# Soft mixture of experts: combine's sums over experts by halves, its first logits fetched into the places of the normed tokens, and the last slot groups and combine in written order

## The chip, the cores and the metric

The kernel runs on one core of one Trainium2 chip. The metric is the time of one execution on the device in microseconds, taken as the median of several runs. The core has a matrix engine (PE), a vector engine (DVE), an activation engine (ACT), a general engine (POOL) and an engine that issues transfers (SP). Each of them runs its own list of instructions in the order of that list, and they meet at semaphores. All arithmetic is in float32.

## The reference

Four layers work on 16 sequences of 128 tokens with 256 features, each layer a gated cross attention and a gated feed-forward part. The change lies in the feed-forward part of layer 2, a soft mixture with 64 experts of 32 slots each:

```python
logits = (jnp.einsum('tzd,ed->tze', x, phi_w) + phi_b).reshape(t, z, n, p)
D = jax.nn.softmax(logits, axis=3)
C = jax.nn.softmax(logits, axis=2)
X_tilde = jnp.einsum('tznp,tzd->npd', D, x)
X_tilde = jnp.clip(X_tilde, -33000.0, 65000.0)
...
X_tilde = (X_tilde - mu) * jax.lax.rsqrt(var + LN_EPS)
X_tilde = jnp.tanh(X_tilde)
Y_tilde = jnp.einsum('npd,ndH->npH', X_tilde, expert_w) + expert_b[:, None, :]
Y = jnp.einsum('tznp,npH->tzH', C, Y_tilde)
```

Here x is the normed input, n = 64 experts and p = 32 slots. So every token has 2048 logits. The same logits are used twice: D is a softmax over the 32 slots of one expert, and C is a softmax over the 64 experts for one slot number. The result Y is scaled by a gate and added to the residual.

## The kernel before

The 2048 tokens are 16 blocks of 128, one token to a partition. The feed-forward part of layer 2 is the function `attention_ffn2`. After the attention of layer 2 it has three stages.

**Dispatch** (`dispatch` and `gather`, lines 1246 to 1288) runs 32 steps: first the logits of the first 1024 columns for all 16 blocks, then those of the other 1024. In a step PE computes two times 512 logits from the transposed normed tokens (`xnT`, four tiles of four blocks each) and the weights `phi`; DVE adds the bias, and SP writes the 1024 logits to a buffer in memory (`spill`). DVE then takes the maximum over the 32 slots (`red`), the maximum over the experts of this half (`top`, line 1266), and subtracts `red`; ACT takes the exponential, DVE sums and inverts, POOL multiplies. Two steps later `gather` multiplies the result on PE with the normed tokens and adds it up in four banks; after the last block of a half ACT copies them to `xtT`.

**Slots** (`slots_norm`, `slots_turn`, `slots_expert`, lines 1182 to 1229) has eight groups of 256 slots. For each group PE turns the slots, DVE clamps them and takes their statistics, POOL computes the inverse root (`rsqrt`, lines 190 to 195), ACT applies tanh, PE turns them again, ACT copies, and PE multiplies with the weights of eight experts. DVE adds the bias to give `yt`. Groups 0 to 3 belong to the first half and are spread over dispatch steps 18 to 29. Groups 4 to 7 come after the last gather. The expert weights (2 MB a group) are loaded into the pool `wp`, which has four places that `phi`, expert weights, fetched logits and the weights of attention 3 share.

**Combine** (`combine`, `turn`, `spread`, lines 1306 to 1342) reads the logits back from memory, two blocks (2 MB) to a place of `wp` (`fetch`, line 1234). For each block DVE subtracts the maximum over the experts (line 1311), ACT takes the exponential in four pieces (line 1315), DVE sums the 2048 values over the 64 experts (line 1317), inverts (1318) and scales (1319). Then each quarter of a block, called a unit here, is turned on PE by four transposes (line 1325), copied by ACT (1329), and multiplied with `yt` in four matrix products (1337). In the profile each product counts as two matmuls. After four units DVE adds the gated result to the residual (line 259). PE spreads a unit two units after it has turned it.

In these stages the order of instructions on each engine is made by a scheduler from priorities, from the order of the program and from free places of the pools; it is not written out. A block `tc.manual_schedule(engines=ENGINES)` fixes the order on PE, ACT, DVE and POOL to the one in which the program states it; the feed-forward part of layer 3 is already written so. Transfers on SP are never part of such a block. Instructions of later stages may still be placed between those of a block: two of these matter here, the preparation of the key mask of attention 3 (line 1632, which needs the mask that line 1628 loads) and the statistics and norm of the residual for attention 3 (lines 199, 201 and 226).

Attention 3 (`xattn64`, lines 269 to 408) follows. Its weights are loaded over POOL's queue into places of `wp`.

## Time and profile before

| What | Value |
|---|---|
| Time before, median of 3 runs | 2056.13 us (2055.76 to 2060.23) |
| Profiled execution, its own time | 2059.8 us |
| Its span, first to last instruction | 2058.1 us |
| PE busy over the span | 1854.9 us (90%) |
| DVE busy | 1257.9 us (61%) |
| ACT busy | 912.3 us (44%) |
| POOL busy | 791.2 us (38%) |
| Granted PE clock, mean | 0.952 |
| Spread matmuls, line 1337 | 126.1 us for 512 |
| Last gather ends, about | 1318.6 us from the start |
| First turn of combine | 1353.07 us |
| First projection of attention 3 (line 287) | 1513.9 us |

Times inside the kernel are counted from the first instruction of the profiled execution. A line of the profile names an engine, a line of the program, an operation, output and inputs, and shapes. Busy time is not the time an engine costs: what counts is who waits last, and the idle time in brackets behind a line names the instruction whose end it was put down to. The column for the PE clock is the share of the full clock that was granted.

### The profile page before, as it was taken

What the parts mean: (1) busy time and instruction counts of PE and PEld (TensorE: products, weight loads), DVE (VectorE), ACT (ScalarE), POOL (GpSimd) and SP (SyncE); (2) the same over time, 40 slices, a digit from 0 to 9 for tenths busy, and PEclk for the clock granted to TensorE, in tenths of its full rate; (3) what the DMA queues carried; (4) which work ended last, traced back from release to release, by engine and by line L of the source; (5) the groups of instructions that cost most, each with busy time, mean ns of one, the idle gap of its engine ahead of it and who ended that gap; (6) DMA issues with size and microseconds to landing.
All of it is one profiled execution on the core that took longest, in us unless ns stands there. A gap on an engine that the chain in (4) does not pass through costs nothing.

```text
span 2058.1 us, 31016 instructions
## 1 busy us (share of the span) xinstructions
PE 1854.9 (90%) x10345; PEld 1242.7 (60%) x10345; DVE 1257.9 (61%) x3763; ACT 912.3 (44%) x3002; POOL 791.2 (38%) x952
## 2 busy tenths in 40 slices
PE   6996899979879999989979989868999999998787
PEld 3774566557636566657744434357776677775775
DVE  3885122478752222249859999699717666663797
ACT  4993222489911222249931122244324434333673
POOL 4873332377510455448832222200102222220785
PEclk9997999998889999999999999989999999999799
DMA  3003777310010688861031123433200000000000
GB/s 118 14 17 111 283 292 283 113 31 27 17 75 1 252 321 315 308 230 37 2 115 79 75 109 143 181 144 120 82 1 1 1 1 1 22 1 1 6 17 21
DMA packets 52720, 204.19 MB, mean 99 GB/s; under 512 B 11600, under 2 KB 31568, under 8 KB 41552
## 3 DMA queue, kind: packets, MB, share of 16 engines
q0 software_dynamic: 13872, 121.12, 16.1%
q1 hardware_dynamic: 38688, 81.07, 11.2%
q8 instruction: 84, 1.38, 0.3%
q14 instruction: 76, 0.62, 0.1%
HBM read 171.75 MB, written 30.41 MB: 98 GB/s over the span
## 4 chain that ended last, share of the span: by engine, by line
PE 27%; DVE 20%; issue 3%; ACT 3%; POOL 2%; DMA 1%; SPq 0%; POOLq 0%; ACTq 0%; DVEq 0%
PE pk L287 3%; PE pq L299 3%; PE po L382 3%; PE pv L310 3%; DVE tot L1317 2%; DVE rep L1523 2%; PE acc L1280 2%; PE po L1337 2%; PE av L372 2%; DVE cw L1311 1%; PE sc L329 1%; PE pq L1419 1%; DVE cw L1319 1%; PE pe L358 1%; PE pl L1254 1%
## 5 line engine op out<-in xcount | busy, mean ns | idle before, releaser
L922 PE MATMUL pg<-we,xT 128*128 128x512 f32 (+1 forms) x528 | 243.1, 590 | 2.4 <-ACT xT L211 2.4
L579 POOL TENSOR_TENSOR e<-e,sums 128x512 f32<-128x512 f32 x192 | 199.6, 1071 | 67.4 <-DVE sums L574 28.4
L928 DVE TENSOR_TENSOR h<-sg,pg 128x256 f32<-128x256 f32 x132 | 54.3, 411 | 237.7 <-ACT sg L927 190.1
L566 ACT ACTIVATE e<-sc,mx 128x128 f32<-128x128 f32 x512 | 181.5, 421 | 17.3 <-DVE mx L544 16.3
L927 ACT ACTIVATE sg<-pg 128x256 f32<-128x256 f32 x132 | 49.7, 376 | 270.3 <-PE pg L922 260.3
L888 POOL DMA_INDIRECT we<-in_we,rows x56 | 54.0, 964 | 265.6 <-PE pd L953 165.2
L350 POOL TENSOR_TENSOR e<-e,rec 128x512 f32<-128x512 f32 x64 | 65.3, 1041 | 219.0 <-DVE rec L349 155.2
L922 PEld LDWEIGHTS pg<-we,xT 128*128 128x128 f32 x528 | 96.2, 194 | 82.2 <-issue 72.1
L1337 PE MATMUL po<-yt,cT 128*128 128x256 f32 x512 | 126.1, 391 | 11.2 <-ACT cT L1329 11.1
L1280 PE MATMUL acc<-d,k 128*128 128x512 f32 x256 | 123.1, 623 | 13.9 <-POOL d L1270 13.5
L566 ACT ACTIVATION_READ_ACCUMULATOR e<-sc,mx 128x1 f32 x512 | 132.9, 260 | 0.0
L585 PE MATMUL pe<-ident,e 128*128 128x128 f32 x768 | 103.7, 279 | 32.0 <-DVE mx L549 17.4
L1270 POOL TENSOR_TENSOR d<-d,tot 128x1024 f32<-128x1024 f32 x32 | 62.8, 1961 | 174.0 <-DVE tot L1269 174.0
L953 PE MATMUL pd<-we,hT 128*128 128x256 f32 x528 | 127.2, 383 | 1.2 <-ACT hT L942 1.2
L1265 ACT ACTIVATE d<-d 128x1024 f32<-128x1024 f32 x32 | 33.8, 1057 | 200.8 <-DVE d L1264 178.9
L953 PEld LDWEIGHTS pd<-we,hT 128*128 128x128 f32 x528 | 98.4, 190 | 40.0 <-issue 23.7
L585 PEld LDWEIGHTS pe<-ident,e 128*128 128x128 f32 x768 | 86.0, 142 | 49.9 <-POOL e L579 24.6
L1254 PE MATMUL pl<-phi,xnT 128*128 128x512 f32 x256 | 116.1, 598 | 0.0
L1337 PEld LDWEIGHTS po<-yt,cT 128*128 128x128 f32 x512 | 95.6, 197 | 23.8 <-ACT cT L1329 12.6
L566 ACT ACTIVATE e<-e,mx 128x128 f32<-128x128 f32 x256 | 99.0, 397 | 0.3 <-DVE mx L549 0.3
L259 DVE SCALAR_TENSOR_TENSOR x<-po,gates,x 128x256 f32<-128x256 f32 x96 | 42.6, 444 | 92.5 <-PE po L382 54.2
L1280 PEld LDWEIGHTS acc<-d,k 128*128 128x128 f32 x256 | 48.9, 199 | 78.7 <-issue 53.3
(304 smaller groups left out, 4361.5 us busy)
## 6 DMA issues: line engine op xcount, KB each, us to landing
ew<-in_ew SPq DMA_DIRECT2D x8, 2048.0 KB
spill<-lg SPq DMA_DIRECT2D x32, 512.0 KB
cw<-spill SPq DMA_DIRECT2D x8, 2048.0 KB
got<-results SPq DMA_DIRECT2D x48, 128.0 KB
normed<-xn SPq DMA_DIRECT2D x32, 128.0 KB
aw<-in_aw SPq DMA_DIRECT2D x6, 512.0 KB
ctxT<-in_ctxT SPq DMA_DIRECT2D x4, 512.0 KB
x<-in_x SPq DMA_DIRECT2D x16, 128.0 KB
```

Source lines behind the costliest of these rows:

```text
L287: nc.tensor.matmul(pk, lhsT=wk[:, k, c * P : (c + 1) * P], rhs=ctxT[g][:, k, :], start=(k == 0), stop=(k == 1))
L299: nc.tensor.matmul(pq[:, i * gt : (i + 1) * gt], lhsT=wq[:, k, (c + i) * P : (c + i + 1) * P], rhs=xnTs[g][:, k, :], start=(k == 0), stop= ...
L350: nc.gpsimd.tensor_tensor(e, e, rec.unsqueeze(2).to_broadcast([P, 4, S]), ALU.mult)
L566: nc.scalar.activation(e[:, c, :], sc[:, c, :], AF.Exp, bias=mx[:, h : h + 1], scale=sign, accum_out=sums[b][:, h : h + 1],)
L579: nc.gpsimd.tensor_tensor(e, e, r, ALU.mult)
L585: nc.tensor.transpose(pe[:, c * P : (c + 1) * P], e[:, c, :], ident)
L922: nc.tensor.matmul(pg[:, 0 : 2 * m].rearrange("p (g i) -> p g i", g=2), lhsT=tokens[j][:, k, :], rhs=wgu[:, k, :, i0 : i0 + m], start=(k = ...
L953: nc.tensor.matmul(pd[:, 0:D], lhsT=hT[0:m, ic, :], rhs=wd[0:m, ic, :], start=(ic == 0), stop=(ic == nic - 1))
L1254: nc.tensor.matmul(pl, lhsT=xnT[b // 4][:, k, tok], rhs=phi[:, k, n], start=(k == 0), stop=(k == 1))
L1270: nc.gpsimd.tensor_tensor(dv, dv, tot.unsqueeze(2).to_broadcast([P, 32, 32]), ALU.mult)
L1280: nc.tensor.matmul(acc[hf][k][q], lhsT=keep[b][:, k * P : (k + 1) * P], rhs=d[:, q * 512 : (q + 1) * 512], start=(b == 0), stop=(b == B - 1),)
L1337: nc.tensor.matmul(pos[b][:, 0:D], lhsT=cT[:, c, :], rhs=yt[2 * q + c // 2][:, c % 2, :], start=(q == 0 and c == 0), stop=(q == 3 and c == 3),
```

## The change

It has five parts.

1. `slots_norm` is split into `slots_gather` (up to the inverse root) and `slots_squash` (from there on).
2. The logits of blocks 0 and 1 are not fetched into `wp`, but in four pieces of 1024 columns into the four places of the normed tokens (`fetch_early`), each as its place comes free in the second half of dispatch. The other blocks are fetched as before, now with one transfer to a block.
3. `combine` is split into four functions. The maximum of the two halves of `top` is taken once for all blocks. The sum over experts adds the two halves of the 2048 columns, then the two halves of the result, and reduces the remaining 512 columns.
4. The last dispatch step, the last gathers, the slot groups 4 to 7, and pieces of combine for blocks 0 and 1 are in one written order.
5. The loop of combine is in a written order too, with the exponentials one piece to a unit, and the shift, the sum and the scaling of a block each at one of the units before it.

```diff
-            def slots_norm(n, dp):
+            def slots_gather(n, dp):
...
                 rsqrt(rs, mv[:, :, 1], 1e-5)
+                xs[n] = t, mv, rs
+
+            def slots_squash(n, dp):
+                t, mv, rs = xs[n]
                 nm = small.tile([P, 2], F32, tag="nm2", name="nm2")
...
+            def fetch_early(b):
+
+                cws[b] = []
+                for h in range(2):
+                    t = xtp.tile([P, 2, GT], F32, tag="xnT", name="cwe").rearrange("p c t -> p (c t)")
+                    nc.sync.dma_start(out=t, in_=spill[b, :, h * 1024 : (h + 1) * 1024])
+                    cws[b].append(t)
+
             def fetch(n):
 
                 cw = wp.tile([P, WSLOT], F32, tag="w", name="cw")[:, 0:4096].rearrange("p (i m) -> p i m", i=2)
-                nc.sync.dma_start(out=cw, in_=spill[2 * n : 2 * n + 2].rearrange("i p m -> p i m"))
                 for i in range(2):
-                    cws[2 * n + i] = cw[:, i, :]
+                    nc.sync.dma_start(out=cw[:, i, :], in_=spill[2 * n + i])
+                    cws[2 * n + i] = [cw[:, i, :]]
...
+            def combine_shift(b):
+                for part in cws[b]:
+                    cv = part.rearrange("t (n p) -> t n p", p=32)
+                    nc.vector.tensor_tensor(
+                        cv, cv, top[:, b, 0, :].unsqueeze(1).to_broadcast([P, cv.shape[1], 32]), ALU.subtract
+                    )
+
+            def combine_exp(b, q):
+                part = logits_of(b, q * 512, 512)
+                nc.scalar.activation(part, part, AF.Exp)
+
+            def combine_sum(b, pool):
+
+                t = pool.tile([P, 1024], F32, tag="lg", name="tree", bufs=2)
+                nc.vector.tensor_tensor(t, logits_of(b, 0, 1024), logits_of(b, 1024, 1024), ALU.add)
+                nc.vector.tensor_tensor(t[:, 0:512], t[:, 0:512], t[:, 512:1024], ALU.add)
+                tots[b] = small.tile([P, 32], F32, tag="tot32", name="tot")
+                nc.vector.tensor_reduce(tots[b], t[:, 0:512].rearrange("t (n p) -> t p n", p=32), AX.X, ALU.add)
+
+            def combine_scale(b):
+                tot = tots.pop(b)
+                nc.vector.reciprocal(tot, tot)
+                for part in cws[b]:
+                    cv = part.rearrange("t (n p) -> t n p", p=32)
+                    nc.vector.tensor_tensor(
+                        cv, cv, tot.unsqueeze(1).to_broadcast([P, cv.shape[1], 32]), ALU.mult
+                    )
...
-                for t in range(2 * B + 2):
-                    if t < 2 * B:
-                        dispatch(t)
+                for t in range(2 * B - 1):
+                    dispatch(t)
...
-                pipeline(4, *(lambda n, stage=stage: stage(4 + n, dp) for stage in slots))
-                fetch(0)
+                    if t == 2 * B - 8:
+                        fetch_early(0)
+
+
+                with tc.manual_schedule(engines=ENGINES):
+                    dispatch(2 * B - 1)
+                    fetch_early(1)
+                    gather(2 * B - 3)
+                    gather(2 * B - 2)
+                    nc.vector.tensor_tensor(top[:, :, 0, :], top[:, :, 0, :], top[:, :, 1, :], ALU.max)
+                    combine_shift(0)
+                    for q in range(4):
+                        combine_exp(0, q)
+                    gather(2 * B - 1)
+                    combine_shift(1)
+                    for q in range(3):
+                        combine_exp(1, q)
+                    combine_sum(0, dp)
+                    for n in (4, 5):
+                        slots_gather(n, dp)
+                    for n in (4, 5):
+                        slots_squash(n, dp)
+                    combine_scale(0)
+                    slots_turn(4, dp)
+                    slots_gather(6, dp)
+                    slots_turn(5, dp)
+                    slots_gather(7, dp)
+                    slots_expert(4, dp)
+                    fetch(1)
+                    for n in (6, 7):
+                        slots_squash(n, dp)
+                    slots_expert(5, dp)
+                    for n in (6, 7):
+                        slots_turn(n, dp)
+                    for n in (6, 7):
+                        slots_expert(n, dp)
...
+                with tc.manual_schedule(engines=ENGINES):
+                    for u in range(4 * B + 4):
+                        b, q = divmod(u, 4)
+                        if q == 0 and b % 2 == 0 and b + 4 < B:
+                            fetch(b // 2 + 2)
+                        if u < 4 * B:
+                            turn(u)
+                        if q == 0 and b + 1 < B:
+                            combine_exp(b + 1, 3)
+                        if q > 0 and b + 2 < B:
+                            combine_exp(b + 2, q - 1)
+                        if 0 <= u - 2 < 4 * B:
+                            spread(u - 2)
+                        if q == 0 and b + 2 < B:
+                            combine_shift(b + 2)
+                        if q == 1 and b + 1 < B:
+                            combine_sum(b + 1, cp)
+                        if q == 2 and b + 1 < B:
+                            combine_scale(b + 1)
+                        if q == 2 and b > 0:
+                            add_gated(b - 1, pos.pop(b - 1)[:, 0:D], gate_f(2))
```

`logits_of(b, at, n)` gives n columns of block b's logits from column `at` on, whichever of the two forms of storage the block has.

More of the change, by code (lines that the diff above doesn't have):

```diff
@@ L1229, in slots_expert, with slots_norm @@
                 nc.vector.tensor_tensor(yt[n], py.rearrange("p (i d) -> p i d", i=2), yt[n], ALU.add)
+            def slots_norm(n, dp):
+                slots_gather(n, dp)
+                slots_squash(n, dp)
             slots = (slots_norm, slots_turn, slots_expert)
             cws = {}
+            def fetch_early(b):
[4 more added lines that the diff above has]
+                    cws[b].append(t)
@@ L1234, in fetch, with logits_of @@
             def fetch(n):
                 cw = wp.tile([P, WSLOT], F32, tag="w", name="cw")[:, 0:4096].rearrange("p (i m) -> p i m", i=2)
-                nc.sync.dma_start(out=cw, in_=spill[2 * n : 2 * n + 2].rearrange("i p m -> p i m"))
                 for i in range(2):
-                    cws[2 * n + i] = cw[:, i, :]
+                    nc.sync.dma_start(out=cw[:, i, :], in_=spill[2 * n + i])
+                    cws[2 * n + i] = [cw[:, i, :]]
+            def logits_of(b, at, n):
+                parts = cws[b]
+                size = 2048 // len(parts)
+                return parts[at // size][:, at % size : at % size + n]
@@ new lines, in attention_ffn2 @@
+            tots = {}
+            def combine_shift(b):
[13 more added lines that the diff above has]
+                nc.vector.tensor_reduce(tots[b], t[:, 0:512].rearrange("t (n p) -> t p n", p=32), AX.X, ALU.add)
@@ L1298, in attention_ffn2 @@
                         gather(t - 2)
-                pipeline(4, *(lambda n, stage=stage: stage(4 + n, dp) for stage in slots))
-                fetch(0)
+                    if t == 2 * B - 8:
[15 more added lines that the diff above has]
+                    for n in (4, 5):
+                        slots_gather(n, dp)
+                    for n in (4, 5):
[8 more added lines that the diff above has]
+                    for n in (6, 7):
+                        slots_squash(n, dp)
+                    slots_expert(5, dp)
[3 more added lines that the diff above has]
+                        slots_expert(n, dp)
@@ L1303, in attention_ffn2 @@
             with tc.tile_pool(name="comb", bufs=3) as cp:
                 cTs, pos = {}, {}
-                def combine(b):
-                    cw = cws[b]
-                    cv = cw.rearrange("t (n p) -> t n p", p=32)
-                    red = cp.tile([P, 32], F32, tag="red", name="red")
-                    nc.vector.tensor_tensor(red, top[:, b, 0, :], top[:, b, 1, :], ALU.max)
-                    nc.vector.tensor_tensor(cv, cv, red.unsqueeze(1).to_broadcast([P, 64, 32]), ALU.subtract)
-                    for q in range(4):
-                        part = cw[:, q * 512 : (q + 1) * 512]
-                        nc.scalar.activation(part, part, AF.Exp)
-                    tot = cp.tile([P, 32], F32, tag="tot", name="tot")
-                    nc.vector.tensor_reduce(tot, cv.rearrange("t n p -> t p n"), AX.X, ALU.add)
-                    nc.vector.reciprocal(tot, tot)
-                    nc.vector.tensor_tensor(cv, cv, tot.unsqueeze(1).to_broadcast([P, 64, 32]), ALU.mult)
@@ L1325, in turn @@
                         nc.tensor.transpose(
-                            pt[:, c * P : (c + 1) * P], cws[b][:, (4 * q + c) * P : (4 * q + c + 1) * P], ident
+                            pt[:, c * P : (c + 1) * P], logits_of(b, (4 * q + c) * P, P), ident
                         )
@@ L1340, in spread @@
                         )
-                    if q == 3:
-                        add_gated(b, pos.pop(b)[:, 0:D], gate_f(2))
-                fetch(1)
-                for b in range(2):
-                    combine(b)
-                for u in range(4 * B + 2):
-                    b, q = divmod(u, 4)
-                    if q == 0:
-                        if b % 2 == 0 and b + 4 < B:
-                            fetch(b // 2 + 2)
-                        if b + 2 < B:
-                            combine(b + 2)
-                    if u < 4 * B:
-                        turn(u)
-                    if u >= 2:
-                        spread(u - 2)
+                with tc.manual_schedule(engines=ENGINES):
+                    for u in range(4 * B + 4):
+                        b, q = divmod(u, 4)
+                        if q == 0 and b % 2 == 0 and b + 4 < B:
+                            fetch(b // 2 + 2)
+                        if u < 4 * B:
[14 more added lines that the diff above has]
+                            add_gated(b - 1, pos.pop(b - 1)[:, 0:D], gate_f(2))
     def attention_ffn3():
```

## The prediction

> **What bounds the kernel now.** I read the page first (PE busy 90% of the span), then the stretches around the changed stage, the timelines of PE and DVE in it, the chain, and the waits of the DMA queue. Busy time per stretch (columns: stretch, length, busy us of PE, weight load, DVE, ACT, POOL, PE clock, DMA share, GB/s):
>
> ```profile
> 1311.00:1338.00 27.00, 19.10 (x168) 10.54 (x168) 9.76 (x32) 8.99 (x16) 5.46 (x9) 0.87 0.38 147
> 1338.00:1353.00 15.00, 0.00 (x0) 0.00 (x0) 15.00 (x13) 4.38 (x8) 0.00 (x0) 0.57 0.81 335
> 1353.00:1470.00 117.00, 104.23 (x552) 90.37 (x552) 117.00 (x79) 51.93 (x98) 0.77 (x2) 0.97 0.24 90
> 1470.00:1514.00 44.00, 43.11 (x217) 37.55 (x218) 12.49 (x27) 12.75 (x23) 6.37 (x17) 0.92 0.13 49
> ```
>
> From 1338 to 1470 DVE is busy without a gap: combine is bound by DVE, PE stands still for 15 us and then waits in places. From 1470 PE works off what is left. PE's timeline:
>
> ```profile
> 1313.51 5.09 PE L1280 MATMUL acc<-d,k 128*128 128x512 f32 x8 [3.11 <-POOL d L1270]
> ...
> 1353.07 2.79 PE L1325 MATMUL pt<-ident,cw 128*128 128x128 f32 x12 [15.50 <-DVE cw L1319]
> ...
> 1470.89 3.78 PE L1337 MATMUL po<-yt,cT 128*128 128x256 f32 x8 [2.97 <-ACT cT L1329]
> ```
>
> The first turn of combine starts at 1353.07, held by the division of DVE. Eight spread matmuls take 3.78 us after an idle gap of 2.97, against 1.73 when fed, which the chain shows:
>
> ```profile
> 1486.60 0.44 PE pt L1325 x4
> 1487.03 1.73 PE po L1337 x8
> ```
>
> So a unit (a quarter of a block) costs PE 2.17 us; 64 units are 138.7 us. The chain hands over to attention 3 at 1513.9: combine takes 160.8. Now DVE ahead of it, and the mask load of attention 3 on SP:
>
> ```profile
> 1305.58 1.90 DVE L1266 TENSOR_REDUCE top<-lg 128x32 f32<-128x1024 f32 x1
> 1307.39 1.21 DVE L1264 TENSOR_TENSOR d<-lg,red 128x1024 f32<-128x1024 f32 x1
> 1309.79 1.22 DVE L1268 TENSOR_REDUCE tot<-d 128x32 f32<-128x1024 f32 x1 [1.18 <-ACT d L1265]
> 1311.05 0.35 DVE L1269 RECIPROCAL tot<-tot 128x32 f32<-128x32 f32 x1
> 1319.08 1.29 DVE L1193 TENSOR_SCALAR xs<-pt 128x512 f32<-128x512 f32 x2 [7.68 <-PE pt L1189]
> ```
> ```profile
> SPq L1628 <- PE acc L1280: 13.9, 1, 13.9
> ```
> ```profile
> 1318.64 0.33 SPq L1628 DMA_DIRECT2D mk<-in_mask_k  x1
> ```
>
> DVE has a hole of 7.68 us while PE ends the dispatch; the mask waits for the last gather.
>
> **Part 1: first blocks of combine into the dispatch tail.** The four early fetches (512 KB each) stand on SP behind spills 18, 22, 26 and 30, and wait for the matmuls of dispatch 19, 23, 27, 31, which end before the logits that the next spill needs: no spill or expert load behind them is held by that wait. Their bytes take 1.3 us each at the 400 GB/s of the fetch stretch. A logits buffer is reused two dispatches (some 15 us) later, and after its start this stage shows no DVE wait on a spill: 0, bounds 0 to 4 x 1.3 = 5.2 us (the one row against is the wait of 8.0 us in the third dispatch, at 1071 to 1079).
>
> In dispatch 31 the written order puts the subtraction ahead of the column maximum. Start to start the maximum is 1.81, and 1.18 was waited for the exponential, so the division is ready some 1.2 us earlier: POOL ends at 1312.1 instead of 1313.45. PE's gap before the last gather falls from 3.11 to about 1.7. Gaps of 2.38 and 2.73 left the matmuls at speed, those of 2.97 and more did not; so I take 3.6 us instead of 5.09 (bounds 3.6 to 5.1) and an end at 1315.7 instead of 1318.6.
>
> DVE meanwhile, from 1310.0: maximum over the halves (512 elements, by the 512-wide add at L1229, 0.6), shifts of blocks 0 and 1 (4 x 1.13, by L1264), the sum of block 0 as 1.13 + 0.6 + 0.95 (a half, a quarter, and a 512-element reduction at the 3.63/2048 of L1317): 7.9 us, in the hole of 7.68. The exponentials (4 x 0.52 on ACT) end at about 1314.1; the copies of the accumulators queue behind them and still end with the last accumulator. The sixteen small maxima of L1310 (0.1 to 0.2 each) go.
>
> **The wait it adds.** In the issue order of the changed kernel one mask preparation (0.15 us, L1632 before) comes on DVE just ahead of that last reduction. It needs the mask, whose load goes out only after the last gather. Queued behind it are the reduction, the clamp of slot group 4, and with it POOL, ACT and PE, which all wait for that group. In the trace before, the bytes moved until between 2.4 and 3.4 us after the issue; the operation itself came 4.2 after (upper bound). I take 3.1, where the bytes have gone: 1318.8 (1318.1 to 1321.4). Then 0.15 + 0.95: the clamp starts at 1320.0, 0.9 later than before, although its input is 2.9 earlier. [...]
>
> **Part 2: slots in written order.** From the clamp, by rows of this stretch (clamp 0.65, statistics 0.85, POOL 1.15 with its latencies, tanh pair 1.09, copies 0.59, sixteen expert matmul pairs 1.93): tanh 4 and 5 end at +4.5 and +5.6; the division of block 0 (0.26 + 2 x 1.13) ends at +7.0 and pushes the clamp of group 6 there; statistics 6 and 7 end at +8.5 and +10.0, tanh 7 at +13.1, expert 6 runs from +13.75, expert 7 ends at +17.6. Before, the same chain took 18.5. First turn: 1337.6 (1336.8 to 1340.1), its division long done. Against 1353.07: **-15.5 us**.
>
> **Part 3: combine.** DVE per block: shift 2.18, sum 1.13 + 0.6 + 0.95 in place of 3.63, reciprocal 0.26, scaling 2.20, gated add 0.39: 7.7, plus 0.43 of attention 3's statistics in blocks 0 to 7, against PE's 8.66. The loop that could bind: turn 0.5, copy 0.65, last exponential 0.6, sum 2.7, scaling 2.5 is 7.0, so a block's division comes 1.6 us before its turn. In four blocks DVE also normalises x (0.33) behind POOL's root, which is ready 1.1 us after the statistics (the 0.65 that L226 waited before, plus the 0.4 of work in between); in blocks 0 and 1 pieces of the sum fill that time, in blocks 2 and 3 nothing does and DVE waits all of it. Followed block by block, slack shrinks to 0.4 and PE stalls 0.6 and 1.0: 1.6 us. ACT has 1.1 us of work per 2.17. Fetches: four slots hold eight blocks; eight megabytes moved in 20 us at 1330 to 1350, and each fetch, now in two issues of 0.36 on SP where nothing else waits, goes out at least two blocks ahead of its shift: 0; the first one leaves at 1328.5, its first megabyte is there by 1333, when DVE gets to it.
> Combine: 138.7 + 1.6 + 0.6 at the start = 140.9 against 160.8: **-19.9 us**. Lower bound 138.7, PE never waiting; upper 152, if DVE takes 9.5 per block: that is the sum of its rows and a fifth more, and I take the rows because each operation has one of its own engine, type and width.
>
> **Part 4: what follows.** PE's order in attention 3 is unchanged, and PE is busy all 86 us of 1514 to 1600. Its first weights now stand on POOL behind eight roots; the last needs block 7's output, at about 1412, and their slot comes free after unit 39, at 1425, fifty us ahead of use: 0, cover being that fifty.
>
> **Sum.** -15.5 - 19.9 = -35.4. The profiled execution (2059.8 us, span 2058.1) is 3.7 above the median of 2056.13; it becomes 2024.4, and the median 2020.7: 2021.
>
> **Rivals.**
> (a) Part of it is lost again: DVE's loop is longer than its rows (dependent short operations, one behind the other), or spills hold the dispatch. For: DVE has 0.5 us to spare per block while statistics run. Against: every duration is from this stage. At 9.5 per block 11 us are lost, with 5.2 in dispatch 16: 2032 to 2037.
> (b) Slower: the division comes so late in each block that PE idles 2.97 us and drops to half clock, as at 1470.89, where two units took 7.3 instead of 4.3: 3.0 idle and 3.0 of slow matmuls, 6 per block. With fifteen blocks: 2021 + 90 = 2111; it decides from six blocks on (35.4/6). The loop must grow from 7.0 to 11.6. [...]
> (c) No change: attention 3 waits for its weights and not for combine. They would have to land 79 us later than worked out: 2056.
> (d) More: the mask is no hindrance and DVE never late: 2017.
>
> **How the numbers follow.** My case 0.74 (2017 to 2026), (a) 0.16, (b) 0.03, (c) 0.02, (d) 0.05. The range of 2015 to 2034 holds the first, (d) and the better part of (a), with the 4 us by which the runs before differ. Faster by over 0.2% (4 us, about what these runs can tell from no change): 0.95; within: 0.02; slower: 0.03.
>
> **What would show it.** Right: no PE gap of 15 us; first turn of combine near 1338 and the chain on PE's turn and spread lines from there to about 1479, units of 2.17, DVE idle for about half a us per block; the mask preparation ahead of a DVE gap of 2 us near 1317. Wrong: PE waiting at every fourth turn on L1289, DVE's waits on spills in dispatch, or first projections of attention 3 waiting on a DMA.

## The result, and the profile after

The changed kernel takes 2034.29 us, the median of 4 runs (2030.32 to 2035.92), against 2055.95 us before: a ratio of 0.9888 with a 95% interval of 0.9876 to 0.9899, or 21.7 us less. That is the right sign, 13 us above the forecast and 0.3 above the upper end of its range; measured again it was 2031.96, inside the range.

The two profiled executions cannot be subtracted as they stand. The dispatch began at 1054.33 us before and at 1049.62 us after, ahead of every instruction that the change touches. So all positions below are counted from the first dispatch matmul of the same execution. The table has every kernel of this study; "forecast" is the prediction's positions less 1054.33. Combine runs from its first turn to the first projection of attention 3.

| Kernel | last gather starts | it takes | clamp, slot group 4 | first turn | attention 3 | combine |
|---|---|---|---|---|---|---|
| before | 259.2 | 5.09 | 264.8 | 298.7 | 459.4 | 160.6 |
| b_again (before) | 259.2 | 5.17 | 264.8 | 298.8 | 459.5 | 160.6 |
| forecast | 257.8 | 3.6 | 265.7 | 283.3 | 424.2 | 140.9 |
| after | 260.5 | 5.40 | 270.1 | 288.2 | 433.0 | 144.9 |
| a_again (after) | 260.6 | 5.40 | 270.5 | 288.6 | 433.4 | 144.9 |
| loop_auto | 260.6 | 5.40 | 270.4 | 288.5 | 430.8 | 142.2 |
| tail_auto | 261.7 | 5.68 | 267.8 | 285.7 | 430.6 | 144.9 |
| mask_early | 259.4 | 6.72 | 268.0 | 287.8 | 432.6 | 144.9 |
| d31_dve | 259.6 | 3.67 | 268.2 | 286.4 | 431.2 | 144.8 |
| block1_ahead | 259.6 | 6.61 | 270.4 | 290.7 | 435.0 | 144.3 |
| sum_whole | 259.0 | 5.16 | 268.4 | 288.0 | 439.9 | 151.8 |
| stats_written | 259.4 | 6.75 | 270.8 | 288.9 | 435.9 | 146.9 |
| halves_alone | 259.3 | 5.20 | 265.0 | 299.3 | 442.0 | 142.8 |
| best | 258.1 | 5.37 | 264.3 | 284.4 | 427.7 | 143.2 |
| best_w | 258.4 | 5.37 | 264.6 | 284.7 | 431.6 | 147.0 |

The stage became 26.4 us shorter (459.4 to 433.0), not 35.4. The 9 us that are missing lie in three places: the gather, the clamp behind it, and combine. Busy time per stretch of the changed kernel, with the columns as in the prediction:

```profile
1308.00:1337.80 29.80, 18.96 (x169) 10.88 (x169) 23.40 (x41) 12.34 (x23) 5.56 (x9) 0.83 0.32 125
1337.80:1400.00 62.20, 57.66 (x321) 49.54 (x318) 57.51 (x62) 30.61 (x56) 5.45 (x10) 1.00 0.40 160
1400.00:1482.60 82.60, 82.60 (x453) 72.15 (x452) 66.08 (x64) 36.86 (x66) 7.43 (x8) 1.00 0.20 77
```

The stretch in which PE stood still for 15 us is gone. From 1400 on PE (first busy figure) is busy without a gap, so combine is PE's there, as forecast; in the 62 us ahead of that it stands for 4.5, while DVE (third figure) is busy for 57.5. The timeline of PE shows where:

```profile
1310.09 5.40 PE L1332 MATMUL acc<-d,k 128*128 128x512 f32 x8 [3.03 <-POOL d L1322]
...
1337.79 1.53 PE L1395 MATMUL pt<-ident,cwe 128*128 128x128 f32 x12
...
1344.42 0.66 PE L1395 MATMUL pt<-ident,cwe 128*128 128x128 f32 x4 [1.09 <-DVE cwe L1289]
...
1381.89 0.66 PE L1395 MATMUL pt<-ident,cw 128*128 128x128 f32 x4 [1.27 <-DVE cw L1289]
1392.04 0.66 PE L1395 MATMUL pt<-ident,cw 128*128 128x128 f32 x4 [1.27 <-DVE cw L1289]
...
1482.65 1.88 PE L287 MATMUL pk<-ctxT,wqk 128*128 128x512 f32 x4
```

The last gather starts after a gap of 3.03 us and takes 5.40 against 3.70 for the one before it; for 3.41 us of it, from 1310.68 on, the granted clock was 0.50. The turns of a new block wait for the scaling on DVE (L1289): the sign that the prediction had named for being wrong. The turns of blocks 2 and 4 wait less (0.2 and 0.7). The first wait of this kind ends 6.6 us after the first turn: PE turns two units ahead of its spreads, so it asks for block 1 after four turns and two spreads, some 5.4 us, and not after the 8.66 of a block.

The tail of dispatch, by the timeline over all engines:

```profile
1301.40 1.91 POOL L1322 TENSOR_TENSOR d<-d,tot 128x1024 f32<-128x1024 f32 x1 [6.74 <-DVE tot L1321]
1302.44 1.95 DVE L1316 TENSOR_TENSOR d<-lg,red 128x1024 f32<-128x1024 f32 x1
...
1307.88 2.16 POOL L1322 TENSOR_TENSOR d<-d,tot 128x1024 f32<-128x1024 f32 x1 [4.56 <-DVE tot L1321]
1308.31 6.21 DVE L1268 TENSOR_TENSOR cwe<-cwe,top 128x1024 f32<-128x1024 f32 x4
...
1315.52 0.33 SPq L1704 DMA_DIRECT2D mk<-in_mask_k  x1
...
1318.62 0.23 DVE L1708 TENSOR_SCALAR mf<-mk 128x128 f32<-128x128 uint8 x1 [2.23 <-DMA mk<-in_mask_k]
1318.76 1.00 DVE L1282 TENSOR_REDUCE tot<-tree 128x32 f32<-128x512 f32 x1
1319.68 0.68 DVE L1193 TENSOR_SCALAR xs<-pt 128x512 f32<-128x512 f32 x1
```

Two things stand here. The mask preparation does what the forecast said, to the tenth: 3.1 us after its load went out. And DVE's subtraction takes 1.95 us where it took 1.21 before, and the four shifts take 6.21 where their rows gave 4.5; both lie across a multiplication on POOL. The subtraction ends 1.08 us after POOL does.

### The profile page after: what moved, and what is told of

It is laid out like the page before. It is cut to its first block, busy times and chain, and to the rows that moved or that the text cites. A ratio compares the mean times of both kernels' runs of the same rounds, so it can differ in the third digit from the quotient of the medians.

```text
span 2028.2 us, 31054 instructions
## 1 busy us (share of the span) xinstructions
PE 1845.2 (91%) x10345; PEld 1236.3 (61%) x10345; DVE 1252.6 (62%) x3784; ACT 912.8 (45%) x3002; POOL 795.3 (39%) x952
## 4 chain that ended last, share of the span: by engine, by line
PE 29%; DVE 17%; issue 3%; ACT 3%; POOL 2%; DMA 1%; SPq 1%; POOLq 0%; ACTq 0%; DVEq 0%
PE po L1407 4%; PE po L382 3%; PE pk L287 3%; PE pq L299 3%; PE pv L310 3%; DVE rep L1599 2%; PE av L372 2%; PE sc L329 2%; PE pq L1495 1%; DVE tot L1320 1%; DVE d L1316 1%; PE pe L358 1%; DVE red L1313 1%; POOL e L579 1%; PE acc L1332 1%
## 5 line engine op out<-in xcount | busy, mean ns | idle before, releaser
L1407 PE MATMUL po<-yt,cT 128*128 128x256 f32 x512 | 120.9, 380 | 0.0
L194 POOL TENSOR_SCALAR ve<-mv 128x1 f32<-128x1 f32 (+1 forms) x136 | 29.9, 220 | 213.3 <-DVE mv L201 168.1
```

Source lines behind the costliest of these rows:

```text
L1407: nc.tensor.matmul(pos[b][:, 0:D], lhsT=cT[:, c, :], rhs=yt[2 * q + c // 2][:, c % 2, :], start=(q == 0 and c == 0), stop=(q == 3 and c == 3),
```

## The experiments

Three questions: what holds the tail (mask, POOL), what made combine shorter (written order, halves, early start), and what stalls PE in it. Most of the changed kernel's variants differ from it by less in time than their intervals allow to tell (0.9876 to 0.9899 and 0.9866 to 0.9899 for the changed kernel itself). What is concluded from them rests on positions and waits in one profiled execution of each; in the two kernels that were profiled twice, positions in the stage repeat within 0.4 us.

### Both kernels again

No edit.

> The changed kernel once more. Question: its profiled execution began the dispatch at 1049.5 us and that of the kernel before at 1054.1, so 4.6 of the 29.5 us between the two profiled executions lie ahead of every instruction that the change touches. Theory (executions scatter ahead of the stage): the stretch from the first dispatch matmul to the first projection of attention 3 repeats at 433 us within 1.5, with one stall of PE at every fourth turn (1.3, 0.3, 0.9, 1.5, 1.5 us) until block 6, while the start of the dispatch comes out anywhere from 1048 to 1055; the median is about 2034. Rival (the change moves what is ahead of it): the dispatch begins at 1049.5 within 0.5 again, and that of the kernel before at 1054.1.

> The kernel before once more. Theory (executions scatter ahead of the stage): from the first dispatch matmul to the first projection of attention 3 it takes 459.8 us within 1.5 again, and the dispatch begins anywhere from 1048 to 1055. Rival (the change moves what is ahead of it): the dispatch begins at 1054.1 within 0.5.

a_again: 2031.96 us, ratio 0.9882 (0.9866 to 0.9899). From dispatch to attention 3 it takes 433.4 again, and the kernel before 459.5 again; the dispatch began at 1052.85 and 1054.74. So the start scatters by 3.2 us for one kernel (by 5.5 over all runs, 1049.6 to 1055.2), and the stage itself repeats within 0.4. The theory holds. Both profiled executions of the kernel before (2059.8 and 2060.28) lie some 4 us above the median of its other runs; where these 4 us are, traces can't show, since only profiled executions have one.

### The loop of combine not in written order

```diff
-                with tc.manual_schedule(engines=ENGINES):
+                with ExitStack():
                     for u in range(4 * B + 4):
```

> The loop of combine is no longer in written order; the early fetches, the tail and the sum by halves stay as in the changed kernel. Theory (written order carries part of the 15.9 us that combine became shorter, the shorter sum and the early start the rest): the shift of later blocks is put ahead of the sum of the next block, the next turn waits for its division, and combine grows from 144.8 us to between 150 and 160; the time is 5 to 15 us above that of the changed kernel. Rival (the shorter work of DVE alone made combine shorter): combine stays within 144 to 147 and the time within 3 us of the changed kernel.

2030.48 us, ratio 0.9871 (0.9850 to 0.9892). Combine takes 142.2, less than in written order: both expectations were wrong, and the written loop costs 2.6 us. DVE's timeline shows two differences. The first is where the statistics stand:

```profile
1449.50 0.39 DVE L199 BATCH_NORM_STATS2 st<-x 128x6 f32<-128x256 f32 x1
...
1455.41 1.98 DVE L226 TENSOR_SCALAR xn<-x,mv,rs 128x256 f32<-128x256 f32 x4 [0.59 <-POOL rs L195]
```

Here the scheduler leaves attention 3's statistics until 1449, when PE has its work and DVE has time. Between the written instructions of the changed kernel they stand from 1357 on, in the blocks in which DVE is behind:

```profile
1371.98 2.28 DVE L1268 TENSOR_TENSOR cw<-cw,top 128x2048 f32<-128x2048 f32 x1
1374.17 0.42 DVE L199 BATCH_NORM_STATS2 st<-x 128x6 f32<-128x256 f32 x1
1374.63 0.18 DVE L201 BATCH_NORM_AGGREGATE mv<-st 128x2 f32<-128x6 f32 x1
1375.76 0.41 DVE L226 TENSOR_SCALAR xn<-x,mv,rs 128x256 f32<-128x256 f32 x1 [0.95 <-POOL rs L195]
1376.09 1.22 DVE L1279 TENSOR_TENSOR tree<-cw 128x1024 f32<-128x1024 f32 x1
1377.34 0.69 DVE L1280 TENSOR_TENSOR tree<-tree 128x512 f32<-128x512 f32 x1
1378.07 1.05 DVE L1282 TENSOR_REDUCE tot<-tree 128x32 f32<-128x512 f32 x1
1379.15 0.35 DVE L1286 RECIPROCAL tot<-tot 128x32 f32<-128x32 f32 x1
...
1382.15 2.28 DVE L1268 TENSOR_TENSOR cw<-cw,top 128x2048 f32<-128x2048 f32 x1
```

From shift to shift such a block takes DVE 10.17 us (1371.98 to 1382.15), against PE's 8.66. The three operations of the sum follow each other at 1.25, 0.73 and 1.08 us, 3.06 in all, since each starts 0.03 to 0.04 us behind the end of the one whose result it reads. The second difference is that in loop_auto another block's work lies between them, and the next operation starts 0.07 to 0.09 us ahead of the end of the one before it; there they take 1.13, 0.61 and 0.96, as the prediction had it:

```profile
1342.36 1.22 DVE L1279 TENSOR_TENSOR tree<-cwe 128x1024 f32<-128x1024 f32 x1
1343.49 2.29 DVE L1268 TENSOR_TENSOR cw<-cw,top 128x2048 f32<-128x2048 f32 x1
1345.69 0.68 DVE L1280 TENSOR_TENSOR tree<-tree 128x512 f32<-128x512 f32 x1
1346.30 1.22 DVE L1279 TENSOR_TENSOR tree<-cw 128x1024 f32<-128x1024 f32 x1
```

PE's waits in combine fall from 4.5 us to 1.8. No run has a written loop with the statistics left to the end, so how the 2.6 us divide between the two is not shown.

### The tail not in written order

```diff
-                with tc.manual_schedule(engines=ENGINES):
+                with ExitStack():
                     dispatch(2 * B - 1)
```

> The dispatch tail and the slots of groups 4 to 7 are no longer in written order; early fetches and the loop of combine stay as in the changed kernel. Here the mask preparation of attention 3 stands behind the slots on DVE and not ahead of the last part of block 0's sum, and the subtraction of dispatch 31 stands behind the column maximum again. Theory (the mask preparation costs the clamp of slot group 4 about 2 us, and the earlier subtraction brought the last gather only 0.3): the clamp of group 4 comes at about 1318 us against 1319.7, and the first turn of combine, 1337.8 in the changed kernel, comes between 1335 and 1338; the time is 0 to 3 us less than that of the changed kernel. Rival (the written order is what holds the first turn at 1338): the first turn comes 3 to 8 us later, and so does the end.

2031.13 us, ratio 0.9889 (0.9869 to 0.9909). The last gather comes 1.1 us later than in the changed kernel and the clamp still 2.3 to 2.7 earlier, since the mask preparation stands behind it (at 279.3). The first turn comes 2.4 to 2.9 earlier. The theory holds for the mask; the rival is refuted: the early fetches and pieces bring the first turn forward without the written order too. The gather is late for two reasons. From POOL's multiplication of dispatch 30 to that of 31 it is 8.4 us here and 6.5 in the changed kernel, since shifts of block 0 and 1 stand ahead of the sum and the reciprocal that it needs; and it takes 0.5 longer. (The step at about 1205 that grew by 1.0 to 1.5 in the changed kernel did not grow here, which hides part of it.) The timeline over all engines shows the second reason:

```profile
1310.17 4.00 DVE L1268 TENSOR_TENSOR cwe<-cwe,top 128x1024 f32<-128x1024 f32 x2
1310.40 2.70 POOL L1322 TENSOR_TENSOR d<-d,tot 128x1024 f32<-128x1024 f32 x1 [6.49 <-DVE tot L1321]
```

Two shifts take 4.00 us instead of 2.3 and POOL 2.70 instead of the 1.91 of the kernel before: they lie across each other from 1310.40 to 1313.10.

### The mask of the first two sequences loaded at the start

```diff
+    first = const.tile([P, 2, S], a["mask_k"].dtype, name="mk2")
+    nc.sync.dma_start(out=first, in_=a["mask_k"][0:2, :].unsqueeze(0).to_broadcast([P, 2, S]))
...
-                nc.vector.tensor_scalar(mf, m[:, b, :], -HUGE, None, ALU.mult)
+                nc.vector.tensor_scalar(mf, first[:, b, :] if b < 2 else m[:, b, :], -HUGE, None, ALU.mult)
```

> The two mask preparations of attention 3 that stand in the dispatch tail on DVE read a small copy of the mask that is loaded at the start of the program; nothing else changes, and nothing is left out. Theory (the wait for the mask holds the clamp of slot group 4): the clamp comes 7.3 to 7.7 us after the start of the last gather instead of 9.59, when block 0's sum ends on DVE, and the first turn of combine lies 286.0 to 286.6 us behind the first dispatch matmul instead of 288.2 to 288.6; combine stays at 144.9; the time falls by about 2 us. Rival (DVE's own work, the shifts above all, sets the clamp): 0.5 us or less.

2032.93 us, ratio 0.9884 (0.9867 to 0.9901): no difference in time that these runs can tell. From the end of the last gather to the clamp it is 1.9 us, against 4.2 and 4.5 in the two executions of the changed kernel, so the wait is gone and was worth 2.3 to 2.6. But the gather took 6.72 in this execution and the second pair of expert products 5.35, and that took the gain (in the changed kernel, at a granted clock of 1.00, the gather before the last takes 3.70 and this pair 3.66): the first turn came 0.4 to 0.8 earlier, not 1.6 to 2.6. The preparation now waits for something else, the last gather, which its timeline names as the releaser (the likely reason is a place in memory that the gather still reads; it was not tried):

```profile
1314.52 6.72 PE L1334 MATMUL acc<-d,k 128*128 128x512 f32 x8 [3.09 <-POOL d L1324]
...
1321.28 0.23 DVE L1710 TENSOR_SCALAR mf<-mk 128x128 f32<-128x128 uint8 x1 [1.19 <-PE acc L1334]
```

### The last dispatch's multiplication on DVE

```diff
-                    nc.gpsimd.tensor_tensor(dv, dv, tot.unsqueeze(2).to_broadcast([P, 32, 32]), ALU.mult)
+                    last = nc.vector if u == 2 * B - 1 else nc.gpsimd
+                    last.tensor_tensor(dv, dv, tot.unsqueeze(2).to_broadcast([P, 32, 32]), ALU.mult)
```

> The last dispatch's multiplication is done by DVE and no longer by POOL; nothing is left out. Theory (a two-input operation of DVE and POOL's multiplication hold each other up, which is why the shifts took 6.21 us and not 4.5, and POOL 2.16 and not 1.91): the multiplication takes 1.2 us on DVE, the four shifts 4.5 to 4.7 us, the last gather starts 259.0 to 259.7 us behind the first dispatch matmul instead of 260.5, PE's gap before it is about 2 us instead of 3.03, so its matmuls take 3.6 us instead of 5.4; the mask's load, the clamp and the first turn come 2.3 to 3 us earlier, and the time falls by 2 to 3 us. Rival (the shifts are slow because they are the first to read what a fetch has written): the shifts take 6.2 us again and the clamp stays where it is within 0.7.

2029.56 us, ratio 0.9871 (0.9855 to 0.9888), not clear of the changed kernel's interval; the first turn comes 1.8 to 2.2 earlier, not 2.3 to 3. Its timeline over DVE and PE:

```profile
1310.99 1.22 DVE L1323 TENSOR_TENSOR d<-d,tot 128x1024 f32<-128x1024 f32 x1
...
1312.36 3.67 PE L1333 MATMUL acc<-d,k 128*128 128x512 f32 x8 [2.14 <-DVE d L1323]
1312.85 4.63 DVE L1268 TENSOR_TENSOR cwe<-cwe,top 128x1024 f32<-128x1024 f32 x4
```

With POOL out of it the shifts take 4.63, the gap is 2.14 and the gather runs at full speed in 3.67: the theory, in each of its numbers up to there. The full speed did not hold: in best and best_w, with the same edit and gaps of 2.07 and 2.14, the gather took 5.37 (the last section shows where the gaps lay). The rival (shifts slow because the fetch has just written their input) is refuted: the same data are read here. The clamp gained 2 and not 3 us: the mask's load went out 2.6 us earlier, but behind its preparation stood now the second addition of the sum too, which the changed kernel does while it waits for the mask.

### Block 1's sum and scaling ahead of the loop

```diff
                     for n in (6, 7):
                         slots_squash(n, dp)
+                    combine_exp(1, 3)
+                    combine_sum(1, dp)
                     slots_expert(5, dp)
+                    combine_scale(1)
```

The same three calls leave the first block of the loop.

> The last exponential, the sum and the scaling of block 1 are written into the slots stage, ahead of combine's loop, and not into its first block; nothing is left out. Theory (PE reaches block 1 after 5.4 us and DVE is bound to be behind from there on, at 10.1 us a block while attention 3's statistics run, against PE's 8.66): the 5.7 us that DVE is ahead now cover that deficit, the five stalls of PE (1.3, 0.3, 0.9, 1.5, 1.5) shrink to 1 us in all, combine falls from 144.9 to between 139.5 and 141, the first turn comes at most 0.7 later, and the time falls by 4 to 5 us. Rival (each stall has its own cause in its own block, a wait for POOL's root or for ACT): the first stall goes, 1.3 us, and the later ones stay: combine 143.6.

2033.18 us, ratio 0.9887 (0.9867 to 0.9907). My theory fell, and the rival came close: combine takes 144.3. The first turn comes 2.2 to 2.6 us later, where I had allowed 0.7; the gather took 6.61 in this execution and the second pair of expert products 5.35, against 3.70 for the gather before it and 3.66 for this pair at a granted clock of 1.00 in the changed kernel. The first stall is gone; then 0.3, 1.3, 1.3 and 1.3 remain. The lead is lost at once: in the written loop the exponentials of block 2 stand on ACT one to a unit, so DVE, which could go on, waits for them (1.35 us at 1352.63, put down to ACT's line 1274), and from there on each block takes 10.17 again. A lead of DVE was worth little here, since the written order of ACT paced it.

### The sum in one reduction again, from block 2 on

```diff
+                if len(cws[b]) == 1:
+                    nc.vector.tensor_reduce(tots[b], cws[b][0].rearrange("t (n p) -> t p n", p=32), AX.X, ALU.add)
+                    return
```

> The sum by halves is undone for the fourteen blocks from block 2 on: one reduction of 2048 elements as in the kernel before (3.63 us there) instead of three operations (3.07 us from start to end); nothing is left out. Theory (DVE is the bound of combine's first blocks and near it in the rest, so the sum by halves carries a good part of the gain): the DVE work of a block rises by 0.56, to 10.7 in blocks with statistics and roots, 9.4 with statistics alone and 8.9 without, all above PE's 8.66; combine grows from 144.9 to between 150 and 153 and the time by 5 to 8 us. Rival (the gain comes from the early start and from what is taken out of combine, the sum is hidden): combine stays within 1.5 us.

2037.88 us, ratio 0.9918 (0.9902 to 0.9935). Combine takes 151.8, within the expectation, and the time rose by 3.6 to 5.9 us. Now PE waits at each of the blocks 1 to 10: 0.3 to 1.1 us in the first four, 2.0 at blocks 5 and 6, ahead of which DVE also waits for POOL's root, and 0.6 in the four after them. PE's timeline:

```profile
1398.04 0.66 PE L1398 MATMUL pt<-ident,cw 128*128 128x128 f32 x4 [2.00 <-DVE cw L1292]
1407.51 0.66 PE L1398 MATMUL pt<-ident,cw 128*128 128x128 f32 x4 [0.59 <-DVE cw L1292]
```

### The halves alone, in the kernel before

```diff
-                    nc.vector.tensor_reduce(tot, cv.rearrange("t n p -> t p n"), AX.X, ALU.add)
+                    t = cp.tile([P, 1024], F32, tag="lg", name="tree", bufs=2)
+                    nc.vector.tensor_tensor(t, cw[:, 0:1024], cw[:, 1024:2048], ALU.add)
+                    nc.vector.tensor_tensor(t[:, 0:512], t[:, 0:512], t[:, 512:1024], ALU.add)
+                    nc.vector.tensor_reduce(tot, t[:, 0:512].rearrange("t (n p) -> t p n", p=32), AX.X, ALU.add)
```

> The kernel before with the sums of combine by halves and nothing else of the change; nothing is left out. Undoing the halves in the changed kernel cost 7 us of combine. Theory (combine of the kernel before is bound by DVE without a gap, so any work taken off DVE comes off its end): sixteen blocks save 0.56 to 0.7 us each, the stretch from the first turn of combine to the first projection of attention 3 falls from 160.6 to between 150 and 153, the first turn comes 0.5 to 1.3 us earlier, and the time is 8 to 12 us below that of the kernel before, close to half of what the change brings. Rival (the planner's order or PE's idle gaps of 2.4 to 3.0 behind ACT's copies bind it): the stretch stays above 156.

2042.88 us, ratio 0.9936 (0.9921 to 0.9952), 13.9 us below the kernel before. Combine takes 142.8 instead of 160.6: 17.8 us, more than I expected and more than the whole change brings in combine. The groups of DVE from 1352 to 1480, first in the kernel before, then here (busy time and mean of one behind the bar):

```profile
L1317 DVE TENSOR_REDUCE tot<-cw 128x32 f32<-128x2048 f32 x14 | 51.7, 3707 | 0.0
```
```profile
L1318 DVE TENSOR_TENSOR tree<-cw 128x1024 f32<-128x1024 f32 x14 | 16.8, 1212 | 0.0
L1320 DVE TENSOR_REDUCE tot<-tree 128x32 f32<-128x512 f32 x14 | 14.2, 1028 | 0.0
L1319 DVE TENSOR_TENSOR tree<-tree 128x512 f32<-128x512 f32 x14 | 9.3, 679 | 0.0
```

For 14 blocks 51.7 us become 40.3, 11.4 us of busy time, and DVE now waits for PE, 12.0 us at the gated add. The rest of the 17.8 was not taken apart; PE's stretches of 3.41 and 6.83 us at a granted clock of 0.50, from 1442.64 and 1469.95 on, belong to it, of which neither is left here (eight spread matmuls took 3.33 and 3.78 us there, and from 1356 on 2.00 at most here). The first turn did not come 0.5 to 1.3 earlier, as expected, but 0.5 later: PE still stands for 15.8 us ahead of it. So the two gains are separate: the early start brings the first turn from 298.7 to about 288.4, the halves bring combine below 143, and the written loop gives 2 to 2.6 of that back, as combine of 144.9 stands against 142.8 here and 142.2 in loop_auto.

### The statistics of attention 3 written out

In the loop each of the first eight blocks takes its statistics right behind its gated add; the first four are normalised behind the shift that follows.

```diff
+                        if q == 0 and 2 <= b < 6:
+                            n3.apply(b - 2)
...
                             add_gated(b - 1, pos.pop(b - 1)[:, 0:D], gate_f(2))
+                            if b - 1 < 8:
+                                n3.stats(b - 1)
```

> The statistics and normalisations of attention 3 that fall into combine stand in the written order: statistics right behind the gated add of a block, its normalisation behind the shift that follows, 2.3 us later; nothing is left out. Writing block 1's sum ahead of the loop did not take the later stalls away, so the theory is now: a block with a normalisation takes DVE 10.15 us against PE's 8.66, and 0.73 to 0.95 of that is DVE's wait for POOL's root. Then the waits on L226 vanish, such a block takes 9.2 to 9.3, the first stall of PE stays (1.3), the three of 0.9 to 1.5 shrink to 0.3 to 0.7 each, and combine falls from 144.9 to 142 to 143.2; the time falls by about 2 us. Rival (DVE's work alone binds these blocks, the wait lies in its slack): combine stays within 0.7.

2036.60 us, ratio 0.9898 (0.9883 to 0.9913), and combine grew to 146.9. My expectation failed, and the trace shows how. The timeline of DVE and POOL:

```profile
1357.33 2.26 DVE L1272 TENSOR_TENSOR cw<-cw,top 128x2048 f32<-128x2048 f32 x1
1357.50 2.14 POOL L194 TENSOR_SCALAR ve<-mv 128x1 f32<-128x1 f32 x1 [22.62 <-DVE mv L201]
1359.72 0.56 POOL L195 TENSOR_TENSOR rs<-ve,nhalf 128x1 f32<-128x1 f32 x1
1360.31 0.41 DVE L228 TENSOR_SCALAR xn<-x,mv,rs 128x256 f32<-128x256 f32 x1 [0.72 <-POOL rs L195]
```

POOL's operation on one number per partition, 0.19 us elsewhere, takes 2.14: it ends 0.05 after DVE's shift. The 2.3 us that I gave the root went into this one operation; PE now waits 1.2 us at each of the blocks 3 to 6. The root then costs DVE 0.72, as before, and block 0's normalisation, which had not waited, waits too.

### Four edits together

Both kernels have the last multiplication on DVE, the small early mask, and block 0's sum behind the first clamps; then `best` has the loop not in written order, and `best_w` has it written with the statistics in it.

```diff
                     for n in (4, 5):
                         slots_gather(n, dp)
+                    combine_sum(0, dp)
```

> The changed kernel with four edits; nothing is left out: the last dispatch's multiplication on DVE, the small copy of the mask loaded at the start, block 0's sum written behind the clamps and statistics of slot groups 4 and 5 and not ahead of them, and the loop of combine not in written order. Theory (these waits lie one behind the other, and the gains add up): the last gather starts 259.6 us behind the first dispatch matmul and takes 3.7, the clamp of group 4 follows at 266.0 to 266.8 (270.1 in the changed kernel), the first turn at 284.2 to 285.2 (288.2 to 288.6), combine takes 142.2, the first projection of attention 3 comes after 426.4 to 427.6 (433.2), and the time is 5 to 7 us below that of the changed kernel, near 2027. Rival (the next wait, for ACT's exponentials of block 1 ahead of the tanh, or for the spilled logits, takes the tail's gain): first turn at 286 to 287, the time 3 to 4 us below.

> The same, but with the loop of combine in written order and the statistics and normalisations of attention 3 written into it. Theory (the root's wait in DVE's order, and not the written order as such, is what made combine 2.7 us longer than without it): the first turn as in the other at 284.2 to 285.2, combine 142 to 143.2, the time within 1.5 us of the other. Rival (the written order itself costs, since DVE may not take the shift that is ready ahead of the sum that is not): combine 144 to 145, and the time 2 to 3 us above the other.

best takes 2027.41 us, ratio 0.9851 (0.9838 to 0.9865); best_w takes 2031.65, ratio 0.9880 (0.9865 to 0.9895). best is the fastest kernel here. Its interval and that of the changed kernel (0.9866 to 0.9899 at the second time) just fail to meet; the stage is 5.4 to 5.8 us shorter. The clamp came at 264.3, earlier than expected; the first turn at 284.4 was within the expectation only because two misses cancelled, since the moved sum met POOL's root: the tanh of group 4 starts 6.7 us after the clamp (1324.65 against 1317.98), and in the changed kernel 3.8. The timeline of best, over all engines:

```profile
1311.86 5.37 PE L1335 MATMUL acc<-d,k 128*128 128x512 f32 x8 [2.07 <-DVE d L1325]
...
1321.58 1.21 DVE L1281 TENSOR_TENSOR tree<-cwe 128x1024 f32<-128x1024 f32 x1
1321.75 1.08 POOL L196 TENSOR_SCALAR ve<-mv 128x2 f32<-128x2 f32 x1 [0.82 <-DVE mv L1200]
1322.82 0.69 DVE L1282 TENSOR_TENSOR tree<-tree 128x512 f32<-128x512 f32 x1
1322.92 1.14 POOL L197 TENSOR_TENSOR rs<-ve,nhalf 128x2 f32<-128x2 f32 x1
```

Between the two, the first turns are 0.3 apart and combine 3.7 (147.0 against 143.2), and the times 4.2. The theory of best_w is refuted. Its rival had the direction, but with 144 to 145 it was too small. The written order together with early statistics costs; which of the two it is, these runs do not separate.

## Why the prediction was right, and by how much it was wrong

The direction and the mechanism were right: PE's 15 us in front of combine and DVE's hold on most of combine both went. The sum was 9 us too large, and the favoured case, 2017 to 2026 with a chance of 0.74, did not come; the time lies at the upper edge of a range that was drawn wider for rival (a). Of the 26.4 us of the stage 1.2 are lost again in layer 3; the 25.2 that are left stand against 21.7 between the medians and 24.7 at the second time. Against a_again, step by step:

- **Fetches early, at no cost.** Right. The dispatch steps keep their lengths, and the only wait on a spill is the one of the third dispatch, far ahead of the first fetch, which the kernel before has too (8.0 us there, 9.7 and 8.4 here). One step, at about 1205, grew by 1.0 to 1.5 us: after a gap of 6.2, which the kernel before has too, more of PE's work fell into a granted clock of 0.50 (5.26 us of busy time, 3.16 in the kernel before), and seven of the nine kernels made from this one, with the same code there, do not have it. DVE's terms in this part add up to 7.8 us, not 7.9.
- **"POOL ends at 1312.1", gap 1.7, gather 3.6.** This step failed: the last gather starts 2.8 later than forecast. The subtraction moved ahead met POOL's multiplication of dispatch 30 (1.95 instead of 1.21), and POOL's next one took 2.16; the last step was 0.3 us shorter, not 1.2. The rest, 1.4, is the step at about 1205. With a gap of 3.08 the gather took 5.40, another 1.8. So the clamp came 4.8 later than forecast.
- **The wait for the mask.** Right: 3.10 after the issue and 3.36 the second time, where 3.1 was taken. From gather to clamp 4.45 us against 4.3.
- **Slots.** 18.1 us from the clamp to the first turn against 17.6; and the division of block 0 is long done by then.
- **Combine, 140.9.** This is the other term that failed: 144.9. PE's idle before the turns adds up to 4.5 us (5.4 counted by the starts of its matmuls) and not 1.6. Three things were priced too low. The sum of a block was priced by operations side by side (2.7) where the written order puts them one behind the other (3.06, plus 0.39 for the reciprocal instead of 0.26). PE asks for block 1 after 5.4 us, not 8.66. And the waits for POOL's root, which the prediction had, fell on blocks without slack.
- **Attention 3 unchanged, 0.** Right for attention 3 itself: its first projection waits for no transfer. From its first projection to the end the kernel takes 1.2 us more in both executions (545.6 and 545.7 against 544.4 twice). In the first of them 0.7 of this lies in the q projections of layer 3, which run at a granted clock of 0.50 for 5.43 us and not 4.07, after a gap of 3.41 in both kernels, and 0.6 in a group of 128x4 products (1.87 us instead of 1.30).
- **Rivals.** The time lies in rival (a), 2032 to 2037 (the second one just below it). Its first mechanism, the loop of DVE longer than its rows, gives the 4.0 us of combine; its second did not come, no spill held the dispatch; and the 4.8 us of the tail no rival had, since none lets POOL and DVE hold each other up. The chance of 0.16 was too low: the prediction itself had counted 0.5 us to spare a block, and the sum and the reciprocal alone take 0.5 more than their rows. Rival (b) did not come: no gap in combine exceeds 1.3 us, and its stretches run at a clock of 1.00. Rival (d) is refuted by the clamp.

What the prediction could not have told from its sum is where the gain comes from. It priced combine as one term; the runs take it apart: the halves alone bring 17.8 us of combine, the early work brings 10.3 at the first turn, and the written loop costs 2.6.

## What to carry to other kernels

Where an engine is the bound, price each operation in the company that it will have: back to back and dependent, not as in a row where other work lay between, and beside what another engine does at that moment. An order written out by hand keeps what is written, but the scheduler still puts other stages' work between it; look for that work in the bound's list before counting on slack. And test the cheapest part of a change alone: here one replaced instruction brought combine more (17.8 us) than all five parts together (15.7).

## What the runs showed of the hardware that was not expected

- **DVE and POOL lengthened each other where an operation of DVE with two inputs lay across one of POOL.** DVE: 1.95 instead of 1.21 (subtraction), 6.21 instead of 4.63 (shifts), 4.00 instead of 2.3; POOL: 2.16 and 2.70 instead of 1.91, and 2.14 and 1.08 instead of 0.19. In these rows the one that came second ended nearly its own duration after the other (the subtraction 1.08, POOL's multiplication of 2.16 us 1.76), or for a tiny operation right behind it (0.05). A reduction with one input was not held up: DVE's of 1.16 us at 1301.18 in the changed kernel ran beside POOL's multiplication, which took its usual 1.91. Why the two lengthen each other no run shows.
- **Half clock did not follow from the length of the gap alone.** After 2.14 us of idle the last gather ran at a granted clock of 1.00 (d31_dve, 3.67 for eight matmuls), after 2.14 in best_w and 2.07 in best it took 5.37 (in best 3.41 of that at 0.50); after 3.03 to 3.11 us it took 5.1 to 6.75 in ten executions. The prediction's reading, that gaps up to 2.73 are harmless and those from 2.97 on are not, came from too few rows. In these traces the granted clock is 1.00 or 0.50 and changes only on a grid with steps of 3.41 us (half clock lasts 3.41, 6.83, 10.24 or 17.07 us in this part of them; in the kernel before and in the changed kernel every change lies on it within 0.001 us). The stretches on this grid show where the gaps lay (columns as in the prediction; best first, then d31_dve):

```profile
1308.85:1312.26 3.41, 1.34 (x4) 0.41 (x3) 3.34 (x5) 0.00 (x0) 0.00 (x0) 1.00 0.93 389
1312.26:1315.67 3.41, 3.41 (x5) 1.35 (x4) 3.38 (x4) 2.06 (x4) 0.00 (x0) 0.50 0.14 58
```
```profile
1307.23:1310.64 3.41, 2.99 (x7) 0.97 (x6) 3.38 (x4) 1.06 (x1) 0.00 (x0) 1.00 0.94 342
1310.64:1314.05 3.41, 1.69 (x4) 0.87 (x5) 3.34 (x5) 0.00 (x0) 0.00 (x0) 1.00 0.60 250
1314.05:1317.46 3.41, 2.31 (x6) 0.71 (x4) 3.41 (x5) 3.35 (x7) 0.00 (x0) 1.00 0.07 28
```

In best the gap lies whole in one step, PE idles 2.07 us of it, and the next step is at half clock. In d31_dve a border of the grid cuts the gap into 0.42 and 1.72, and the steps behind both stay full. The gap of 2.73 in the kernel before was cut in the same way (1.25 and 1.48); of its gap of 3.01, 2.92 lay in one step. Counted from 1060 to 1500 us in all fourteen traces: all 75 steps at full clock in which PE idled 2.03 us or more were followed by half clock; of the 1579 with 1.96 or less, three were, all three at the turns of slot groups 6 and 7. The kernel before and the changed kernel have 13 of the first kind and 221 of the second, none of them an exception. (PE's busy time is modelled, so the limit of about 2 us is an estimate from these counts.) What makes the clock follow these steps no run shows.
